# Attention with projections: the transposing transfers of the softmax sums move to ScalarE's queue

## The chip, the cores and the metric

The kernel runs on one core of a Trainium2 chip. Its five engines (TensorE for matmuls, VectorE, ScalarE, GpSimd, and SyncE, which here only issues transfers) each work through their own list of instructions in order and wait for one another through semaphores. The metric is the device time of one execution in microseconds (us). A profiled execution is a little longer than an unprofiled one, so profiles are compared with profiles and times with times. In the profile's rows PE is TensorE, PEld its weight loads, DVE VectorE, ACT ScalarE, POOL GpSimd, SPq the transfers that SyncE issues and ACTq those that ScalarE issues. L939 is line 939 of the kernel.

## What is computed

One attention block on a picture of 48 x 48 = 2304 positions with 512 channels and a batch of 4, in 8 heads of 64 channels. Cut to what matters:

```python
hn  = group_norm(x, gn_scale, gn_bias)                 # 32 groups
qkv = einsum('oc,bchw->bohw', qkv_w, hn) + qkv_b       # fp32, then rounded to fp16
q, k, v = (qkv[:, i] for i in range(3))                # each (b, 8, 64, 2304)
w   = einsum('bhct,bhcs->bhts', q * scale, k * scale)  # scale = 64 ** -0.25
w   = softmax(w, axis=-1)
a   = einsum('bhts,bhcs->bhct', w, v)
out = x + einsum('oc,bchw->bohw', proj_w, a) + proj_b
```

## The kernel before

The kernel takes two heads at a time: 16 pairs of heads, each with five blocks of columns (positions t), four of 512 columns and a last one of 256. The exponentials of a block are made in *bursts* of three tiles of 128 x 1024. A block of 512 columns has six bursts, the one of 256 has three, and a pair has 27. Projections for later pairs and for the output ("pieces") are put between the bursts, so that TensorE is always busy.

The softmax's sums don't come from TensorE. VectorE adds up the exponentials (`add`), which leaves for each column 128 partial sums, one in each partition. A transposing transfer (`turn`) moves them so that VectorE can reduce them along a row (`sum_up`); then come the reciprocal and a detour through DRAM that spreads it over the partitions (`invert`, `spread`), and GpSimd's multiplication (`divide`).

```python
ppool = tile_pool(name="ppool", bufs=3)               # exponentials, one buffer a burst
ps_s  = tile_pool(name="ps_s", bufs=3, space=PSUM)    # scores, one buffer a tile
ps_w  = tile_pool(name="ps_w", bufs=1, space=PSUM)    # projections: one bank
...
def scores(u):
    ...
    for r in range(BURST):                            # BURST = 3
        ps = ps_s.tile([P, 2, QB], F32, tag="ps")
        ...                                           # 2 (or 4) matmuls into ps
        nc.scalar.activation(pt[:, r], ps, AF.Exp)
...
def add(u):                                           # "acc", and at the block's end "j"
    ...
    nc.vector.tensor_tensor(t, before, pt, ALU.add)
    if last:
        whole = work.tile([P, 1, 2, QB], F16, tag="joined", bufs=1)
        ...                                           # two additions of 128 x 1024
...
def turn(g, j):
    t = work.tile([P, 2 * QB // P, P], F16, tag="turned", bufs=1)
    (whole,) = acc.pop((g, j))
    nc.sync.dma_start(t, whole.rearrange("p a h q -> p (a h q)"), transpose=True)
    turned[g, j] = t

def sum_up(g, j):                                     # L1038 (512 columns), L1041 (256)
    sm = small.tile([P, 2, QB // P], F32, tag="sums")
    ...
    nc.vector.tensor_reduce(sm, t[:, :, :, 0], AX.X, ALU.add)
...
def invert(g, j):
    nc.vector.reciprocal(inv[:, :, :per], sums[g, j][:, :, :per])
    row = dram.tile([2, QB], F32, tag="row")
    for h in range(2):                                # writes of 4 bytes each
        nc.sync.dma_start(row[h, :n].rearrange("(i p) -> p i", p=P), inv[:, h, :per])

def spread(g, j):                                     # one row over 64 partitions
    ib = work.tile([P, QB], F32, tag="ib", bufs=1)
    for h in range(2):
        nc.sync.dma_start(ib[h * D : (h + 1) * D, :n], row[h : h + 1, :n].to_broadcast((D, n)))

def divide(g, j):
    nc.gpsimd.tensor_tensor(atts[g][:, o : o + n], avx[g, j], ibs[g, j], ALU.mult)
```

The order in which each engine gets its work, burst by burst (`n` counts the bursts of all pairs; `block_at(m)` is the block that ended with burst `m`, if one did):

```python
for n in range(end):
    ...                               # loads and stores that are due
    if block_at(n - 3):
        turn(*block_at(n - 3))
    ...
    scores(stream[n])                 # TensorE and ScalarE, burst n
    add(stream[n - 1])                # VectorE
    values(stream[n - 2])             # TensorE; copies av out at a block's end
    fill(n)                           # small VectorE tasks, then projection pieces
    if block_at(n - 4):
        sum_up(*block_at(n - 4)); check_sums(...); invert(...)
    if block_at(n - 6):
        spread(*block_at(n - 6))
    if block_at(n - 7):
        divide(*block_at(n - 7))
```

A piece of the projections is a chain of matmuls into the one bank of `ps_w`, which VectorE empties (k and q at L719, v at L768, the output's residual sum `r` at L864).

Of the kernel before, what the change touches and what calls it, by code (L numbers as in the profile page):

```python
# [33 lines left out]
BEHIND = 2  # L34
# [10 lines left out]
NQ = len(QBLOCKS)  # L45
# [422 lines left out]
def fast_path(  # L468
# [12 lines left out]
    nc = tc.nc  # L481
# [438 lines left out]
    def scores(u):  # L920
        g, j, k, _ = u
        o, n = QBLOCKS[j]
        per = QB // n
        qt, kt = qk[g]
        pt = ppool.tile([P, BURST, 2, QB], F16, tag="p", name=f"p_{g}_{j}_{k}")
        for r in range(BURST):
            ps = ps_s.tile([P, 2, QB], F32, tag="ps", name=f"ps_{g}_{j}_{k}_{r}")
            for a in range(per):
                i = (k * BURST + r) * per + a
                for h in range(2):  # L930
                    rows = slice(h * D, (h + 1) * D)
                    nc.tensor.matmul(  # L932
                        ps[:, h, a * n : (a + 1) * n],
                        kt[rows, bass.ts(i, P)],
                        qt[rows, o : o + n],
                        start=True,
                        stop=True,
                    )
            nc.scalar.activation(pt[:, r], ps, AF.Exp)  # L939
        pts[u] = pt  # L940
# [27 lines left out]
    def add(u):  # L968

        g, j, k, last = u  # L970
        pt = pts[u]
        if k == 0:
            acc[g, j] = [pt]
            return
        if j >= NQ - 2 and g == NG - 1 and (last or j == NQ - 1):
            acc[g, j].append(pt)
            return
        before = acc[g, j][0]
        if k == 1:
            acc[g, j] = [  # L980
                work.tile(
                    [P, BURST, 2, QB], F16, tag="acc", bufs=1, name=f"acc_{g}_{j}"
                )
            ]
        t = acc[g, j][0]
        nc.vector.tensor_tensor(t, before, pt, ALU.add)  # L986
        if last:
            whole = work.tile([P, 1, 2, QB], F16, tag="joined", bufs=1, name=f"j_{g}_{j}")
            so_far = t[:, 0]
            for r in range(1, BURST):  # L990
                nc.vector.tensor_tensor(whole[:, 0], so_far, t[:, r], ALU.add)
                so_far = whole[:, 0]
            acc[g, j] = [whole]
# [30 lines left out]
    def turn(g, j):  # L1024


        t = work.tile([P, 2 * QB // P, P], F16, tag="turned", bufs=1, name=f"t_{g}_{j}")
        (whole,) = acc.pop((g, j))
        nc.sync.dma_start(t, whole.rearrange("p a h q -> p (a h q)"), transpose=True)
        turned[g, j] = t  # L1030

    def sum_up(g, j):

        o, n = QBLOCKS[j]
        sm = small.tile([P, 2, QB // P], F32, tag="sums", name=f"sums_{g}_{j}")
        t = turned[g, j].rearrange("p (h a i) k -> p h i a k", h=2, i=n // P)
        if n == QB:
            nc.vector.tensor_reduce(sm, t[:, :, :, 0], AX.X, ALU.add)  # L1038
        else:
            for h in range(2):  # L1040
                nc.vector.tensor_reduce(sm[:, h, : n // P], t[:, h], AX.XY, ALU.add)  # L1041
        sums[g, j] = sm
# [21 lines left out]
    def check_sums(g, j):  # L1064
        n = QBLOCKS[j][1]
        sm = sums[g, j][:, :, : n // P]
        ok = fine.rearrange("p (h i) -> p h i", h=2)[:, :, : n // P]
        for op, limit in ((ALU.is_ge, SUM_MIN), (ALU.is_le, SUM_MAX)):
            t = small.tile([P, 2, QB // P], F32, tag="in", name=f"in_{g}_{j}")
            t = t[:, :, : n // P]  # L1070
            nc.gpsimd.tensor_scalar(t, sm, limit, None, op)  # L1071
            nc.gpsimd.tensor_tensor(ok, ok, t, ALU.mult)  # L1072

    def invert(g, j):
        n = QBLOCKS[j][1]
        per = n // P
        inv = small.tile([P, 2, QB // P], F32, tag="inv", name=f"inv_{g}_{j}")
        nc.vector.reciprocal(inv[:, :, :per], sums[g, j][:, :, :per])
        row = dram.tile([2, QB], F32, tag="row", name=f"row_{g}_{j}")
        if (g, j) in turned:  # L1080
            for h in range(2):
                nc.sync.dma_start(  # L1082
                    row[h, :n].rearrange("(i p) -> p i", p=P), inv[:, h, :per]
                )
        else:
            nc.sync.dma_start(
                row[:, :n].rearrange("h (p i) -> p h i", i=per), inv[:, :, :per]
            )
        rowd[g, j] = row

    def spread(g, j):
        n = QBLOCKS[j][1]
        row = rowd.pop((g, j))
        ib = work.tile([P, QB], F32, tag="ib", bufs=1, name=f"ib_{g}_{j}")
        for h in range(2):
            nc.sync.dma_start(
                ib[h * D : (h + 1) * D, :n], row[h : h + 1, :n].to_broadcast((D, n))
            )
        ibs[g, j] = ib

    def divide(g, j):
        o, n = QBLOCKS[j]
        nc.gpsimd.tensor_tensor(  # L1103
            atts[g][:, o : o + n],
            avx.pop((g, j))[:, :n],
            ibs.pop((g, j))[:, :n],
            ALU.mult,
        )
# [37 lines left out]
    def do_tasks(room):  # L1146
        while tasks and tasks[0][0] <= now[0] and room > 0:
            _, us, run = tasks.popleft()
            run()
            room -= us  # L1150
# [18 lines left out]
    def ready(b, j):  # L1169

        if b < B - 1:
            return BEHIND + 7
        return BEHIND + (4 if j == NQ - 3 else 6)

    def put_convert(b, j):
        end = ends[((b + 1) * NPAIR - 1) * NQ + j]
        put(projs[b, j][0], end + ready(b, j))
# [130 lines left out]
    def issue():  # L1308
        us, run = beside.pop(0)[:2]
        run()  # L1310
        credit[0] -= us

    def fill(n):

        idle = beside and beside[0][4] and not beside[0][4]()
        if ended(n - 1):
            room = 1.1 if idle else 0.0  # L1320
        elif ended(n - 4):
            room = 1.1 if idle else 0.3
        else:
            room = 2.4 if idle else 1.1
        do_tasks(room)
        rate, work = 0.0, 0.0
        for us, _, _, _, _, _, need in beside:
            work += us
            left = min(need * per_pair, len(stream) - 4) - n
            rate = max(rate, work / max(left, 1))  # L1330
        credit[0] = min(credit[0] + rate, 4.0)
        closed = False
        while beside:
            us, _, first, last, when, after, _ = beside[0]
            if after > n or (first and closed) or (when and not when()):
                break
            if us > 0.1 and credit[0] < us / 2:
                break
            issue()
            closed = closed or last  # L1340

    def wanted(g):

        while any(p[6] <= g for p in beside):
            while loads:
                loads.popleft()[1]()
            while tasks:
                tasks.popleft()[2]()
            issue()
            credit[0] = max(credit[0], 0.0)  # L1350

    ended = lambda n: 0 <= n < len(stream) and stream[n][3]
# [5 lines left out]
    def block_at(n):  # L1358

        return stream[n][:2] if ended(n) and n not in soon else None  # L1360

    for n in range(end):
        now[0] = n
        while loads and loads[0][0] <= n:
            loads.popleft()[1]()
        if block_at(n - 3):
            turn(*block_at(n - 3))
        wanted(stream[n][0])
        scores(stream[n])
        if n > 0:  # L1370
            add(stream[n - 1])
        if n >= BEHIND:
            values(stream[n - BEHIND])
        fill(n)

        if block_at(n - 4):
            sum_up(*block_at(n - 4))
            check_sums(*block_at(n - 4))
            invert(*block_at(n - 4))
        if block_at(n - 6):  # L1380
            spread(*block_at(n - 6))
        if block_at(n - 7):

            divide(*block_at(n - 7))
        if n - BEHIND in soon:
            g, j = stream[n - BEHIND][:2]
            sx = rows(g, j, add_up(g, j))
            if n - BEHIND == soon[1]:
                divide_here(g, j, sx, avx[g, j], nc.gpsimd)
        if n - BEHIND - 1 == soon[0]:  # L1390
            check_sums(g, j)
            invert(g, j)
        if n - BEHIND - 2 == soon[0]:
            spread(g, j)
            divide(g, j)
    g, b, j = NG - 1, B - 1, NQ - 1
    n = QBLOCKS[j][1]
# [99 lines left out]
```

## Time and profile before

| | |
|---|---|
| time, median of 3 runs | 1739.31 us (1738.06 to 1740.24) |
| span of the profiled execution | 1777.9 us |
| mean clock granted to TensorE in it | 0.959 of full speed |
| bursts | 432 |
| transposing transfers | 77, all issued by SyncE |
| exponentials, 128 x 1024 | 1296, mean 1026 ns |
| transfers of reciprocals into DRAM rows | 155 |

A row of the profile's list of groups gives line, engine, operation, what is written from what, the shape and the count; then the busy time, the mean duration of one in ns, and the idle time just before with what ended most of it. The list of waits names the waiting engine and line, then what it waited for, the total in us, the number of times and the longest. A row of the timeline has the start, the duration, the engine, the line and the operation; in brackets stand the idle time before it and what ended it. The duration of a transfer's command is the time in which it was issued, not the time until its data had landed; the latter can be read in the chain of waits, where a DMA row lasts until its data let the next instruction start.

### The profile page before, as it was taken

What the parts mean: (1) busy time and instruction counts of PE and PEld (TensorE: products, weight loads), DVE (VectorE), ACT (ScalarE), POOL (GpSimd) and SP (SyncE); (2) the same over time, 40 slices, a digit from 0 to 9 for tenths busy, and PEclk for the clock granted to TensorE, in tenths of its full rate; (3) what the DMA queues carried; (4) which work ended last, traced back from release to release, by engine and by line L of the source; (5) the groups of instructions that cost most, each with busy time, mean ns of one, the idle gap of its engine ahead of it and who ended that gap; (6) DMA issues with size and microseconds to landing.
All of it is one profiled execution on the core that took longest, in us unless ns stands there. A gap on an engine that the chain in (4) does not pass through costs nothing.

```text
span 1777.9 us, 27819 instructions
## 1 busy us (share of the span) xinstructions
PE 1609.6 (91%) x11316; PEld 700.4 (39%) x11316; DVE 1193.8 (67%) x1317; ACT 1285.4 (72%) x1398; POOL 340.2 (19%) x419
## 2 busy tenths in 40 slices
PE   7999999999999977899999999669999989987677
PEld 2533434433335334453333443335333335334344
DVE  5277677777676766766767667667676767655565
ACT  3287777888878865676878788548787878876575
POOL 1011212221121211112223121111222231210111
PEclk9999999999999997999999999879999999999789
DMA  6012151211111367613111115562312212168534
GB/s 201 1 43 53 22 84 27 32 25 22 37 22 31 72 107 108 108 25 34 25 34 25 31 31 107 109 120 45 40 25 30 29 22 25 34 115 130 85 54 127
DMA packets 206718, 101.97 MB, mean 57 GB/s; under 512 B 162676, under 2 KB 172788, under 8 KB 206580
## 3 DMA queue, kind: packets, MB, share of 16 engines
q1 hardware_dynamic: 204548, 98.25, 31.5%
q8 instruction: 90, 1.47, 0.5%
q10 hardware_dynamic: 1904, 1.84, 0.3%
q14 instruction: 48, 0.39, 0.1%
q0 software_dynamic: 128, 0.01, 0.0%
HBM read 60.70 MB, written 19.17 MB: 45 GB/s over the span
## 4 chain that ended last, share of the span: by engine, by line
PE 62%; DMA 21%; DVE 10%; issue 3%; ACT 2%; SPq 2%; POOL 0%; DVEq 0%; ACTq 0%; POOLq 0%
PE pqk L709 20%; PE ps L932 12%; PE av L957 12%; PE pv L760 11%; DMA t<-j 10%; DMA r<-x_dram 7%; PE pr L837 6%; DVE acc L986 3%; DMA row<-inv 2%; DMA x<-x_dram 2%; DVE sums L1038 2%; ACT p L939 1%; PE ps L709 1%; DVE r L864 1%; SPq L1082 1%
## 5 line engine op out<-in xcount | busy, mean ns | idle before, releaser
L939 ACT ACTIVATE p<-ps 128x1024 f16<-128x1024 f32 x1296 | 1232.3, 1026 | 432.1 <-PE ps L932 419.5
L709 PE MATMUL pqk<-x,wqkv 128*64 128x512 f32 (+1 forms) x2464 | 526.8, 558 | 29.3 <-DVE k L719 14.8
L986 DVE TENSOR_TENSOR acc<-acc,p 128x3072 f16<-128x3072 f16 x270 | 488.2, 1808 | 34.1 <-ACT p L939 31.1
L932 PE MATMUL ps<-q,k 64*128 64x512 f16 (+1 forms) x2880 | 366.0, 364 | 6.6 <-ACT p L939 5.9
L957 PE MATMUL av<-p,v 128*64 128x512 f16 (+1 forms) x2880 | 364.5, 367 | 1.9 <-DVE avx L966 1.5
L760 PE MATMUL pv<-wqkv,x 128*64 128x256 f32 x2304 | 271.3, 383 | 12.4 <-DVE v L768 11.9
L709 PEld LDWEIGHTS pqk<-x,wqkv 128*64 128x64 f32 x2464 | 172.8, 139 | 253.3 <-issue 166.4
L1103 POOL TENSOR_TENSOR att<-avx,ib 128x512 f16<-128x512 f32 (+1 forms) x78 | 122.4, 1570 | 714.6 <-DMA ib<-row 669.2
L932 PEld LDWEIGHTS <-k 64*128 64x128 f16 x2880 | 108.2, 95 | 321.7 <-issue 274.9
L837 PE MATMUL pr<-a,whi 128*128 128x512 f32 (+1 forms) x312 | 134.5, 437 | 96.1 <-DVE r L864 93.1
L1071 POOL TENSOR_SCALAR in<-sums 128x8 f32<-128x8 f32 (+1 forms) x158 | 92.2, 584 | 655.3 <-DVE sums L1038 437.5
L957 PEld LDWEIGHTS <-v 128*64 128x64 f16 x2880 | 126.6, 109 | 215.3 <-issue 176.3
L760 PEld LDWEIGHTS pv<-wqkv,x 128*64 128x64 f32 x2304 | 161.9, 138 | 103.9 <-DVE v L768 14.8
L986 DVE TENSOR_TENSOR acc<-p,p 128x3072 f16<-128x3072 f16 x79 | 140.3, 1776 | 17.5 <-ACT p L939 16.4
L864 DVE SCALAR_TENSOR_TENSOR r<-pr,bproj,r 128x512 f32<-128x512 f32 (+1 forms) x80 | 54.8, 693 | 131.8 <-DMA r<-x_dram 84.9
L837 PE MATMUL pr<-a,wlo 128*128 128x512 f32 (+1 forms) x312 | 125.6, 408 | 0.0
L837 PEld LDWEIGHTS pr<-a,whi 128*128 128x128 f32 x312 | 65.6, 210 | 136.5 <-DVE r L864 74.2
L1072 POOL TENSOR_TENSOR fine<-fine,in 128x8 f32<-128x8 f32 (+1 forms) x158 | 114.5, 725 | 13.2
L719 DVE TENSOR_SCALAR q<-pqk,bqkv 128x512 f16<-128x512 f32 (+1 forms) x79 | 54.8, 694 | 82.4 <-PE pqk L709 81.9
L768 DVE TENSOR_TENSOR v<-pv,bv 128x512 f16<-128x512 f32 x72 | 49.6, 689 | 88.3 <-PE pv L760 82.6
L719 DVE TENSOR_SCALAR k<-pqk,bqkv 128x512 f16<-128x512 f32 (+1 forms) x75 | 52.2, 696 | 70.7 <-PE pqk L709 69.5
L966 DVE COPY avx<-av 128x512 f32<-128x512 f32 (+1 forms) x79 | 49.9, 631 | 53.8 <-PE av L957 48.7
(66 smaller groups left out, 526.9 us busy)
## 6 DMA issues: line engine op xcount, KB each, us to landing
r<-x_dram SPq DMA_DIRECT2D x72, 256.0 KB
out_dram<-r SPq DMA_DIRECT2D x69, 256.0 KB
ib<-row SPq DMA_DIRECT2D x126, 128.0 KB
x<-x_dram SPq DMA_DIRECT2D x62, 256.0 KB
x<-x_dram SPq DMA_DIRECT2D x16, 128.0 KB
row<-inv SPq DMA_DIRECT2D x124, 2.0 KB
ib<-row SPq DMA_DIRECT2D x30, 64.0 KB
wqkv<-qkv_wT_dram SPq DMA_DIRECT2D x2, 768.0 KB
```

The costliest lines, as they stand in the source:

```text
L709: nc.tensor.matmul(pw[0][lo : lo + D, :n], wqkv[:, c, w0 + lo : w0 + lo + D], hn[b, c, j], start=(c == 0), stop=(c == NC - 1),)
L719: nc.vector.tensor_scalar(qk[g][part][:, o : o + n], pw[0][:, :n], bqkv[:, col : col + 1], SCALE, ALU.add, ALU.mult,)
L760: nc.tensor.matmul(pw[0][lo : lo + D, a, :], hn[b, c, i * P // QB][:, at + lo : at + lo + D], wqkv[:, c, 2 * C + half * C // 2 :][:, : C / ...
L837: nc.tensor.matmul(ps[:, :n], w[:, c, bass.ts(m, P)], at32[b, j, c], start=(i == 0), stop=(i == len(steps) - 1),)
L864: nc.vector.scalar_tensor_tensor(xt[:, i], places[i], bias, xt[:, i], ALU.add, ALU.add)
L932: nc.tensor.matmul(ps[:, h, a * n : (a + 1) * n], kt[rows, bass.ts(i, P)], qt[rows, o : o + n], start=True, stop=True,)
L939: nc.scalar.activation(pt[:, r], ps, AF.Exp)
L957: nc.tensor.matmul(av[0][lo : lo + D, :n], vv[b, pr // 2][:, i, pr % 2 * P + lo : pr % 2 * P + lo + D], pt[:, r, h, a * n : (a + 1) * n], ...
L986: nc.vector.tensor_tensor(t, before, pt, ALU.add)
L1071: nc.gpsimd.tensor_scalar(t, sm, limit, None, op)
L1072: nc.gpsimd.tensor_tensor(ok, ok, t, ALU.mult)
L1103: nc.gpsimd.tensor_tensor(atts[g][:, o : o + n], avx.pop((g, j))[:, :n], ibs.pop((g, j))[:, :n], ALU.mult,)
```

## The change

The transposing transfers go into ScalarE's list instead of SyncE's. There they stand ahead of the exponentials of the burst that is three after their block's last one. Everything that hangs on them follows one burst later: VectorE's sums with GpSimd's check and the reciprocal, the spreading, the division, and the moment at which the output's projection may take the block. The amount of small tasks that VectorE gets in the burst of the sums is moved along. The purpose is to take the transposing transfer out of the queue in which it stands behind scattered writes and waiting transfers, and to give it time to land before VectorE reaches the sum.

```diff
@@ def turn(g, j)
-        nc.sync.dma_start(t, whole.rearrange("p a h q -> p (a h q)"), transpose=True)
+        nc.scalar.dma_start(t, whole.rearrange("p a h q -> p (a h q)"), transpose=True)
@@ def ready(b, j)
         if b < B - 1:
-            return BEHIND + 7
-        return BEHIND + (4 if j == NQ - 3 else 6)
+            return BEHIND + 8
+        return BEHIND + (4 if j == NQ - 3 else 7)
@@ def fill(n)
         if ended(n - 1):
             room = 1.1 if idle else 0.0
-        elif ended(n - 4):
+        elif ended(n - 5):
             room = 1.1 if idle else 0.3
@@ for n in range(end)
-        if block_at(n - 4):
-            sum_up(*block_at(n - 4))
-            check_sums(*block_at(n - 4))
-            invert(*block_at(n - 4))
-        if block_at(n - 6):
-            spread(*block_at(n - 6))
-        if block_at(n - 7):
-            divide(*block_at(n - 7))
+        if block_at(n - 5):
+            sum_up(*block_at(n - 5))
+            check_sums(*block_at(n - 5))
+            invert(*block_at(n - 5))
+        if block_at(n - 7):
+            spread(*block_at(n - 7))
+        if block_at(n - 8):
+            divide(*block_at(n - 8))
```

## The prediction

> **What bounds the kernel now.** I read the page first, then the waits, then the stretch around one short block in the order of time. The page's engine shares and the chain:
>
> ```profile
> PE 1609.6 (91%) x11316; PEld 700.4 (39%) x11316; DVE 1193.8 (67%) x1317; ACT 1285.4 (72%) x1398; POOL 340.2 (19%) x419
> ...
> PE 62%; DMA 21%; DVE 10%; issue 3%; ACT 2%; SPq 2%; POOL 0%; DVEq 0%; ACTq 0%; POOLq 0%
> ```
>
> TensorE works 91% of 1777.9 us, so everything that a change can win lies in its 168 us of idle time (26 of them in the first 100 us and after 1740). The list of waits says who ends that idle time:
>
> ```profile
> PE pr L837 <- DVE r L864: 93.1, 15, 9.1
> ...
> DVE sums L1041 <- DMA t<-j: 61.6, 13, 9.3
> ...
> PE pqk L709 <- DVE k L719: 14.8, 7, 4.0
> ...
> PE pv L760 <- DVE v L768: 11.9, 5, 3.8
> ...
> PE pqk L709 <- DVE q L719: 11.0, 5, 4.6
> ...
> DVE sums L1038 <- DMA t<-j: 4.2, 3, 1.9
> ```
>
> The 93.1 us are projections waiting for VectorE to add a residual that is still loading; the change doesn't aim there. The next three TensorE rows are waits for VectorE to empty a PSUM bank. Their origin is the DVE row of 61.6 us: VectorE stands still for the turned sums of the pair's last block (L1041 is the form for 256 columns), 13 times, up to 9.3 us. One of them in the order of time (start, duration, engine, line):
>
> ```profile
> 379.29 1.21 DVE L1038 TENSOR_REDUCE sums<-t 128x8 f32<-128x1024 f16 x1
> ...
> 380.76 0.93 SPq L1082 DMA_DIRECT2D row<-inv  x2
> ...
> 381.42 0.48 DVE L719 TENSOR_SCALAR k<-pqk,bqkv 128x256 f16<-128x256 f32 x1 [0.39 <-PE pqk L709]
> ...
> 381.73 1.23 SPq L1029 DMA_TRANSPOSE t<-j  x1
> ...
> 392.08 1.28 DVE L1041 TENSOR_REDUCE sums<-t 128x2 f32<-128x512 f16 x2 [3.29 <-DMA t<-j]
> ...
> 395.14 0.74 DVE L719 TENSOR_SCALAR q<-pqk,bqkv 128x512 f16<-128x512 f32 x1
> ...
> 395.94 1.94 PE L709 MATMUL pqk<-x,wqkv 128*64 128x512 f32 x8 [1.61 <-DVE q L719]
> ...
> 398.24 2.85 ACT L939 ACTIVATE p<-ps 128x1024 f16<-128x1024 f32 x3 [2.22 <-PE ps L932]
> ```
>
> The last block has three bursts instead of six, so its transposing transfer (381.73) comes on SyncE right behind the previous block's two scattered writes (380.76). It lands some 10.3 us after its issue, VectorE has waited 3.29 us for it, then empties the bank late, and TensorE loses 1.61 us, ScalarE with it.
>
> How late depends on what stands ahead in the queue. In the chain of waits a transfer behind such writes takes 9.35 to 11.5 us, one without them 4.5 to 6:
>
> ```profile
> 263.14 10.00 DMA row<-inv
> ...
> 381.73 10.33 DMA t<-j
> ...
> 619.65 4.46 DMA t<-j
> ...
> 892.54 6.06 DMA t<-j
> ```
>
> **What the Trainium skill says.** "DMA: Bandwidth & Descriptors", section "Queues, rings and completion order": SyncE and ScalarE each own one row of rings on the same 16 DMA engines, and each engine goes round-robin between rows. So in ScalarE's row the transpose needn't wait behind SyncE's 4-byte writes. The two groups of landing times above fit a queue that holds it up. The same page, "Issuing engines are not separate DMA queues", says that a second issuer saves only the issuing time; taken strictly that speaks against a faster landing (a rival below). "Perfetto Trace Analysis", section on the DVE and Act engine instruction: an activation is pushed into a wait queue and the sequencer goes on to the next instruction, so a command may be handled while earlier activations run. Its section on the HWDGE DMA instruction: the sequencer itself waits for a transfer's semaphores and is taken until the descriptors are made. The trace has 1.25 us (median of 77) for that on SyncE; ScalarE issues nothing in its steady state here, so its share isn't shown.
>
> **The change part by part.** The number and form of all compute instructions stay, and so does TensorE's order; 77 transposes move from SyncE's list into ScalarE's, three bursts after their block ended, ahead of that burst's exponentials; the sums move one burst down VectorE's list, behind one more addition and often one more bank.
>
> *Taken away.* I went through the DVE waits for t and added the TensorE gaps that follow within 14 us, nearly all with VectorE emptying a bank as releaser: 1.4, 2.9, 1.6, 3.7, 1.7, 4.0, 2.4, 2.4, 3.8, 3.2, 4.6 and 3.1, together 34.8 us for twelve short blocks. The thirteenth (9.35 us wait, 8.6 us gap) is among the projections; 93.1 / 15 = 6.2 us is usual there, so I count 2.5. Two of the L1038 waits have gaps of 1.4 and 1.3: count 2. Together 39 us. A burst is 3.25 us where projections run beside it, which with the lost queue (10.3 down to about 5 or 6) covers waits of 3.2 to 6.2 us. I take all of it off.
>
> *Added, one: a wait of ScalarE.* The tile t has one buffer. The short block's transpose must follow the sum over the block before. That sum used to stand a burst earlier; now it stands at the end of the burst right ahead of this transpose, in 11 of 15 pairs directly after the emptying of a bank. From the end of TensorE's chain: 0.1 + 0.75 (k, 694 to 750 ns) + 1.21 (the sum) = 2.1 us, then 1.25 us of issuing: the next exponential starts 3.35 us after the chain's end. Now it starts 0.45 after (0.38 to 0.45 in the timeline). There are three score tiles, so TensorE needs the third of the burst free 3.25 + 0.55 us after the chain's end, and three exponentials take 2.86: a start up to 0.9 costs nothing, one at 3.35 costs 2.4. Where two pieces of projection stand in that burst (as at 382.73, 3.60 us), or a projection's wait, most of it is swallowed. I count 8 pairs at 1.7, 3 at 0.5 and 4, with no bank in between, at 0.4: 17 us.
>
> *Added, two: the issuing itself.* 77 x 1.25 = 96 us of ScalarE's sequencer, against 28% of idle ScalarE. For the 62 transposes of long blocks the sums joined are 3 to 6 us old and t is free. If the sequencer runs ahead, one exponential or two (0.95 us each) hide the issue. If not, the start moves from 0.45 to 1.4 and costs 0.5: 31 us at most. I weigh full exposure with a quarter: 8 us.
>
> *Moved.* Row writes, broadcast and division come a burst later. In the projection stages a residual behind row writes takes 11 to 13 us; as many row writes stand among as many residual loads as before, only one place later. I count 0, plus or minus 10. The tail isn't touched: the last block that is turned has its division at 1724.2 and its conversion at 1735.0.
>
> Sum: -39 + 17 + 8 + 0 = -14 us, so about 1725 us.
>
> **The rivals.** (1) *The full gain.* The wait on t's buffer is mostly swallowed and the issue hidden: -39 to -45, 1697 us. For it: ScalarE is only 72% busy. Against it: in the very bursts concerned it has 0.4 us of slack in 3.25. (2) *ScalarE as the new wait.* It isn't able to run ahead, every transpose blocks 1.25 us and the short ones over 3: -39 + 31 + 26 = +18, 1757 us; with slower issuing than on SyncE still more. For it: the queue is in order and TensorE has only three score tiles. Against it: TensorE's mean burst is about 3.8 us (1640 us by 432 bursts) while the exponentials need 2.86. (3) *The landing stays slow* at 10 us, because the same 16 engines are busy with the small writes. Then the added burst of 3.25 us still takes away most of the waits of 3.2 to 4.2, but not those over 5: some 12 us of gain are missing, 1737 us. (4) *The gain is given back to the residuals.* SyncE reaches its loads at the same time, TensorE reaches its projections earlier and waits longer for them: the 93 us become 105. It is inside my plus or minus 10.
>
> **Range and chances.** 1725 us, with 1702 to 1752 for 8 in 10: its lower end is the full gain with little given back, its upper end nearly rival (2). 2% are 34.8 us: under 1704.5 needs nearly all of the gain and none of the two additions, 0.12; over 1774 needs exposed issuing much above 1.25 us or ScalarE waiting for other transfers, 0.06; within 2%, 0.82.
>
> **What would show it.** *Right:* the row of DVE waiting for t, 61.6 us, falls below 10; transposes of short blocks are issued 2 us after the chain's end and have landed within 6 or 7; TensorE's 38 us of waits for k, q and v shrink; a new row appears, ScalarE's exponential or its transposing command waiting for DVE sums, some 1 to 2 us in each of 10 or more pairs, with TensorE's scores waiting for ScalarE (5.9 us now) at 15 to 30. *The issuing:* the gap between exponentials before and after a transpose of a long block, 0.4 us if hidden, 1.4 or more if not. *Wrong:* if that gap is far above 1.4, or DVE's wait for t stays above 30, or the projections' 93.1 us move by more than 15.

## The result: slower by 1.5%

| kernel | time, median | ratio to the kernel before, 95% interval |
|---|---|---|
| before | 1738.68 us (1735.41 to 1740.24, 4 runs) | |
| changed | 1764.36 us (1762.93 to 1765.55, 4 runs) | 1.015 [1.0132, 1.0167] |

About 26 us are lost where 14 were to be won. The change did what it was made for, and something else took more than that back.

One caution on levels. The kernel before takes 1738.7 us on the chip of this table and 1764.4 us on the chip of most experiments below, 1.5% apart for the same program. The profile of before that was shown above has a span of 1777.9 us and belongs to neither level. Profiling as such is not the reason: the changed kernel's profiled execution took 1765.15 us, within its range in the table. So ratios are formed on one chip only, and the trace of the change is compared with a repeat of the kernel before (`e0_before_again`) from the same chip as the repeat of the change (`e4_after_again`).

### The profile page after: what moved, and what is told of

Its sections match the earlier page's. It is cut to its first block, busy times and chain, and to the rows that moved or that the text cites. A ratio compares the mean times of both kernels' runs of the same rounds, so it can differ in the third digit from the quotient of the medians.

```text
span 1763.4 us, 27868 instructions
## 1 busy us (share of the span) xinstructions
PE 1613.5 (91%) x11316; PEld 703.9 (40%) x11316; DVE 1185.7 (67%) x1317; ACT 1284.1 (73%) x1398; POOL 359.0 (20%) x419
## 4 chain that ended last, share of the span: by engine, by line
PE 69%; DMA 13%; DVE 8%; ACT 4%; issue 4%; ACTq 1%; SPq 1%; POOL 0%; DVEq 0%; POOLq 0%
PE pqk L709 22%; PE av L957 14%; PE ps L932 13%; PE pv L760 12%; PE pr L837 6%; DMA r<-x_dram 5%; ACT p L939 4%; DMA row<-inv 3%; DMA t<-j 3%; DVE sums L1038 2%; DVE acc L986 2%; PE ps L709 1%; DMA out_dram<-r 1%; DVE r L864 1%; ACTq L1029 1%
## 5 line engine op out<-in xcount | busy, mean ns | idle before, releaser
L986 DVE TENSOR_TENSOR acc<-acc,p 128x3072 f16<-128x3072 f16 x270 | 478.9, 1774 | 74.5 <-ACT p L939 72.3
L932 PE MATMUL ps<-q,k 64*128 64x512 f16 (+1 forms) x2880 | 369.8, 362 | 48.0 <-ACT p L939 47.3
L957 PE MATMUL av<-p,v 128*64 128x512 f16 (+1 forms) x2880 | 369.6, 371 | 5.6 <-DVE slx L1048 4.2
L1071 POOL TENSOR_SCALAR in<-sums 128x8 f32<-128x8 f32 (+1 forms) x158 | 87.4, 553 | 653.4 <-DVE sums L1038 482.3
L864 DVE SCALAR_TENSOR_TENSOR r<-pr,bproj,r 128x512 f32<-128x512 f32 (+1 forms) x80 | 54.8, 694 | 132.0 <-PE pr L837 59.0
L1072 POOL TENSOR_TENSOR fine<-fine,in 128x8 f32<-128x8 f32 (+1 forms) x158 | 137.1, 867 | 13.2
```

Source lines behind the costliest of these rows:

```text
L864: nc.vector.scalar_tensor_tensor(xt[:, i], places[i], bias, xt[:, i], ALU.add, ALU.add)
L932: nc.tensor.matmul(ps[:, h, a * n : (a + 1) * n], kt[rows, bass.ts(i, P)], qt[rows, o : o + n], start=True, stop=True,)
L957: nc.tensor.matmul(av[0][lo : lo + D, :n], vv[b, pr // 2][:, i, pr % 2 * P + lo : pr % 2 * P + lo + D], pt[:, r, h, a * n : (a + 1) * n], ...
```

## The profile after

The page of the changed kernel, its engine shares and its chain of waits:

```profile
PE 1613.5 (91%) x11316; PEld 703.9 (40%) x11316; DVE 1185.7 (67%) x1317; ACT 1284.1 (73%) x1398; POOL 359.0 (20%) x419
...
PE 69%; DMA 13%; DVE 8%; ACT 4%; issue 4%; ACTq 1%; SPq 1%; POOL 0%; DVEq 0%; POOLq 0%
```

The chain has moved: DMA down from 21% to 13%, ScalarE up from 2% to 4% (on one chip, `e0_before_again` and `e4_after_again`, from 20% to 16% and from 1% to 4%), and ScalarE's sequencer (ACTq) is in it with 1%. Which waits stand behind that is read from the lists of waits of the two kernels on one chip. First the kernel before:

```profile
PE pr L837 <- DVE r L864: 87.0, 15, 8.4
...
DVE sums L1041 <- DMA t<-j: 57.1, 13, 8.7
...
PE pqk L709 <- DVE k L719: 13.4, 6, 3.6
...
PE pv L760 <- DVE v L768: 10.8, 5, 3.5
...
PE pqk L709 <- DVE q L719: 9.4, 5, 3.7
...
PE ps L932 <- ACT p L939: 4.5, 10, 0.5
```

and then the changed kernel:

```profile
PE pr L837 <- DVE r L864: 71.1, 14, 7.9
...
ACT p L939 <- issue: 57.7, 15, 7.5
...
PE ps L932 <- ACT p L939: 50.2, 65, 7.4
...
DVE avx L966 <- POOL att L1103: 20.9, 12, 5.3
...
PE av L957 <- DVE avx L966: 7.4, 4, 2.8
...
DVE sums L1041 <- DMA t<-j: 6.7, 6, 2.5
...
PE av L957 <- DVE slx L1048: 5.0, 1, 5.0
...
PE pv L760 <- DVE v L768: 2.4, 5, 0.8
...
PE pqk L709 <- DVE k L719: 1.8, 4, 1.0
...
PE pqk L709 <- DVE q L719: 0.6, 3, 0.2
```

VectorE's wait for t is gone (57.1 to 6.7 us), and with it TensorE's waits for k, q and v. In their place ScalarE's exponentials wait 57.7 us for nothing that the profile names ("issue": here its own sequencer, held at a transfer's command), and TensorE's scores wait 50.2 us for ScalarE. Two smaller rows are new as well: VectorE copies av out late because GpSimd's division, a burst later, still reads the tile (20.9 us), and TensorE waits for that.

The balance of this pair, TensorE's gaps between 100 and 1740 us summed from the rows of the timeline by what ended them (0.1 us beside the lists here and there):

| TensorE waits for | before | changed | difference |
|---|---|---|---|
| k, q, v out of the bank | 36.9 | 6.4 | -30.5 |
| the residual sums r | 87.3 | 71.0 | -16.3 |
| the exponentials | 4.6 | 50.2 | +45.6 |
| avx, slx (copies of av and of its sums) | 1.7 | 12.4 | +10.7 |
| all gaps | 130.5 | 140.1 | +9.6 |
| TensorE's busy time | 1608.5 | 1616.7 | +8.2 |

The spans are 1763.9 and 1782.7 us, 18.8 apart; the table holds 17.8 of it.

Two stretches of the changed kernel's timeline, from the profile with the page above, show how a transposing transfer stands among the exponentials, first a long block's, then a short block's:

```profile
374.33 1.02 ACT L939 ACTIVATE p<-ps 128x1024 f16<-128x1024 f32 x1 [0.39 <-PE ps L932]
...
374.85 1.25 ACTq L1029 DMA_TRANSPOSE t<-j  x1
...
375.25 1.94 ACT L939 ACTIVATE p<-ps 128x1024 f16<-128x1024 f32 x2
...
387.81 1.21 DVE L1038 TENSOR_REDUCE sums<-t 128x8 f32<-128x1024 f16 x1
...
389.05 1.31 ACTq L1029 DMA_TRANSPOSE t<-j  x1
...
390.46 5.61 ACT L939 ACTIVATE p<-ps 128x1024 f16<-128x1024 f32 x6 [3.46 <-issue]
...
393.36 0.39 PE L932 MATMUL ps<-q,k 64*128 64x512 f16 x2 [0.51 <-ACT p L939]
...
400.20 1.27 DVE L1041 TENSOR_REDUCE sums<-t 128x2 f32<-128x512 f16 x2
```

For the long block the command (374.85) starts while the first of three exponentials runs, and the next two follow without a gap: issuing is hidden. For the short block the command (389.05) comes 0.03 us after the sum over the block before has ended (387.81 + 1.21), and so it is at all fifteen short blocks of `e4_after_again`: it has waited for the one buffer of t, and ScalarE's next exponential stands still for 3.46 us. The sum over the short block at 400.20 then waits for nothing, 11.15 us after the command.

## The experiments

They ran on three chips: the runs from e0 to e7 on one on which the kernel before took 1764 us, e8 to e10 on another of the same level (1763.9 us), the last on a third. "TensorE waits for exponentials" and the like are sums as in the table above, on each run's own trace.

**The kernel before, again.** No edit; it gives the trace to compare with.

> The kernel before, unchanged, profiled once more. The first profile of it had a span of 1777.9 us beside times of 1739 us; that of the changed kernel had 1763.4 us beside 1764. Theory A (the profiled execution of before was later than its timed ones because transfers landed later in it, so that its 61.6 us of VectorE waiting for the turned sums are not what a timed execution has): another profile has a span near 1739, VectorE's wait for t under 25 us, and TensorE's waits for k, q and v together under 20 instead of 38. Theory B (the profile was typical and the change itself costs 25 us somewhere else): the span is again about 1778 and the waits are the same.

Measured 1764.35 us, ratio 1.0002 [0.9985, 1.0019]; span 1763.9, granted clock 0.961. Theory A falls: VectorE's wait for t is 57.1 us, TensorE's for k, q and v 37.0. The waits that the prediction built on are typical. The span of 1763.9 us fits neither theory.

**The changed kernel, again.** No edit; is the loss the same on the other chip?

> The changed kernel, unchanged, beside many runs of the kernel before on one and the same chip. In the first three experiments' call the kernel before itself took 1764.5 us where it had taken 1738.7 for the result. Theory A2 (the chip or its state makes 1.5% of the kernel's time, and the change itself is nearly neutral, its gain of about 54 us in TensorE's waits for VectorE given back in about 43 us of waits for ScalarE): 0.995 to 1.003 of the kernel before in this call. Theory A1 (the change costs 1.5% on any chip): 1.012 to 1.018.

Measured 1784.8 us, 1.0122 [1.0098, 1.0145]. The loss belongs to the change and not to a chip.

**The later burst alone.** The changed kernel, transposing transfers back on SyncE:

```diff
-        nc.scalar.dma_start(t, whole..., transpose=True)
+        nc.sync.dma_start(t, whole..., transpose=True)
```

> The changed kernel with the transposes back in SyncE's queue, so only the burst of delay is left. Theory A (what costs is ScalarE, which stands in its own queue until the sum over the long block before is made, 3.3 us in each pair, while the waits for t were small in timed executions): 1725 to 1742 us, at or below the kernel before, and no gaps of 3.3 us between exponentials. Rival C (the later sums, divisions and conversions cost the 25 us, whatever queue issues): 1755 to 1770 us. Rival D (residual loads fall into a worse place behind the row writes): TensorE's waits for VectorE at L864 above 80 us.

Measured 1769.25 us, 1.003 [1.0018, 1.0043]. Theory A, with the kernel before or below, is out, and so is rival C, since the later burst alone costs 5 us and not 25; rival D's sign (80.0 us at L864) says nothing, with 87.0 in the kernel before. A burst more does not cure the wait here, since SyncE too must wait for t's buffer; it issues later, and VectorE then waits a second time, for the joined tile that the transfer reads:

```profile
DVE sums L1041 <- DMA t<-j: 36.3, 12, 7.1
...
DVE j L991 <- DMA t<-j: 26.6, 10, 7.8
```

TensorE's waits for k, q and v are 37.0 us, as before the change; those for avx and slx 9.7 us instead of 1.7. That is what the later burst brings by itself.

**ScalarE's queue alone.** The kernel before with only the other line of the change:

```diff
-        nc.sync.dma_start(t, whole..., transpose=True)
+        nc.scalar.dma_start(t, whole..., transpose=True)
```

> The kernel before with only the queue changed; sums stay four bursts after their block. ScalarE then finds t free earlier in the short blocks, but the sum over the short block itself comes a burst earlier. Theory A: ScalarE's stalls at the short blocks shrink from 3.3 to about 1 us, VectorE waits for t a little (10 to 30 us in all), time 1740 to 1755. Rival E (issuing from ScalarE costs as such): 1760 or more, with gaps of 1.3 us or more at the long blocks too.

Measured 1752.28 us, 0.9929 [0.9905, 0.9952]. VectorE's wait for t falls to 39.0 us (10 to 30 were expected), TensorE waits 11.1 us for exponentials. So 0.7% is won by one half of the change, 0.3% lost by the other, and 1.2% lost by the two together: the loss lies in how they act on each other.

The trace of this run takes a belief of the prediction away. In the twelve cases in which VectorE waits for a short block's transfer, the time from the command to the sum's start is the landing time. It is 9.4 to 11.2 us on SyncE's queue (`e0_before_again`, without the one at 1105 us, among the loads) and 9.9 to 12.8 us on ScalarE's. The other queue does not make it land sooner; VectorE only waits less because the command goes out earlier.

**The fourth block's sum back in its old burst.** The changed kernel; only the long block just ahead of the short one gets its sum, check and reciprocal a burst earlier, so that t is free when ScalarE comes to the short block's transfer:

```diff
-        if block_at(n - 5):
-            sum_up(...); check_sums(...); invert(...)
+        for due in (4, 5):
+            found = block_at(n - due)
+            if found and (due == 4) == (found[1] == NQ - 2):
+                sum_up(*found); check_sums(*found); invert(*found)
```

> The changed kernel with one thing put back: the sum over the fourth block, which has to free t for the short block's transpose, is again four bursts after its block. Theory A: the 3.3 us stalls of ScalarE at the short blocks fall to under 1, TensorE's waits for exponentials fall from 47 to about 15 us, and the time falls by 20 to 35 us to 1730 to 1745. Rivals C and E: it stays within 8 us of 1764.

Measured 1757.26 us, 0.996 [0.9948, 0.9972], against 1.0122 with the sum late: 1.6% by this one edit. The 3.3 us stalls at short blocks are gone from the trace, VectorE's wait for t stays small (7.3 us), and TensorE's wait for exponentials falls from 50.2 to 28.4 us, not to 15. Of what is left most stands in the stages in which the next picture is loaded, and looks the same as in the changed kernel: exponentials that wait 6.0 and 7.8 us at 618 and 650 us.

**The picture's loads off SyncE.** Those remaining stalls needed a cause. One of them in the timeline of the changed kernel (`e4_after_again`):

```profile
652.55 2.50 SPq L1096 DMA_DIRECT2D ib<-row  x2
...
656.20 2.55 SPq L512 DMA_DIRECT2D x<-x_dram  x4
...
658.67 1.25 ACTq L1029 DMA_TRANSPOSE t<-j  x1
659.20 1.26 POOL L1103 TENSOR_TENSOR att<-avx,ib 128x512 f16<-128x512 f32 x1 [15.72 <-DMA ib<-row]
660.02 2.85 ACT L939 ACTIVATE p<-ps 128x1024 f16<-128x1024 f32 x3 [7.54 <-issue]
661.10 0.61 PE L932 MATMUL ps<-q,k 64*128 64x512 f16 x2 [7.41 <-ACT p L939]
```

The transposing command starts 0.53 us before GpSimd begins to use `ib`, the broadcast that SyncE issued at 652.55 and that has nothing to do with t. The compiled program's own list of waits says why (cut to the transfers between the two). DMAHW0 to DMAHW7 are the eight completion semaphores, counters that a transfer raises when its data has landed; the transfers of SyncE and ScalarE take them in turn:

```
SyncE    ib_1   <- row_1    [waits DMAHW6, DMAHW4, Pool]
SyncE    ib_1   <- row_1    [waits DMAHW7, DMAHW5]
SyncE    r_0_0  <- x_dram   [waits PE]
SyncE    r_0_1  <- x_dram   [waits PE]
SyncE    x_0_3  <- x_dram   [waits DMAHW0]
SyncE    x_1_3  <- x_dram   [waits DMAHW1]
SyncE    x_2_3  <- x_dram   [waits DMAHW2]
SyncE    x_3_3  <- x_dram   [waits DMAHW3]
ScalarE  t_2    <- j_2      [waits DMAHW5, DMAHW4, DVE]
```

A transfer waits until the last user of its semaphore has landed. The transposing transfer is the eighth after the first half of the broadcast and takes the same one, DMAHW4.

The trace holds this wait too, as an instruction of ScalarE's sequencer ahead of each of the 77 commands (the durations are the shortest, the median and the longest in ns):

```profile
L1029 ACTq EVENT_SEMAPHORE  x77: 17/38/8079, 103.4 to 1706.0; - x77
```

The one of this place waits from 650.57 to 658.63, and the last update of DMAHW4, the landing of the broadcast's first half, stands at 658.61. The longest (1091.68 to 1099.76) ends in the same way with a broadcast that landed at 1099.74. At the third long stall, which ends at 628.19, the eighth transfer before is the write of the previous block's reciprocals: it landed at 625.82, and the command started at 625.91. Four smaller stalls at long blocks (131, 237, 260 and 1075 us, with 6.4 us of TensorE after them) also end with the landing of such a write.

If the shared semaphore costs the time, taking the loads out of the count must help the changed kernel, and must do next to nothing for the kernel before:

```diff
 def load_block(b, j):
     for c in range(NC):
-        load_x(b, j, c, nc.sync)
+        load_x(b, j, c, nc.gpsimd)
```

> The changed kernel with the later batches' input loads issued by GpSimd instead of SyncE. Each SyncE or ScalarE transfer reuses the completion semaphore of the one eight transfers earlier, and in the stages with input loads that is the previous block's spreading transfer, still in flight: ScalarE stood 8.3, 6.5 and 5.4 us there. With the loads off these semaphores the eighth transfer back is an old one. Theory F (that is what ScalarE waits for): the three stalls fall below 2 us, TensorE's waits for exponentials fall from 47 to about 30 us, time 8 to 17 us less than the changed kernel in the same call. Rival G (ScalarE waits there for the joined sums or for t): the stalls stay.

> The same for the kernel before, to tell what the input loads' queue does without ScalarE's transposes. Theory F: within 6 us of the kernel before (its transposes are in SyncE's list, where nobody computes). If it gains 10 us or more, then the shorter SyncE queue is what helps the run before this one too.

> The input loads issued by GpSimd and the fourth block's sum four bursts after its block, both on the changed kernel: no ScalarE stall over 2 us should be left at the short blocks or in the loading stages. Theories A and F together: TensorE's waits for exponentials under 15 us, 0.98 to 0.99 of the kernel before. If it isn't below the run with the early sum alone (0.996), F falls.

Measured: 1.0038 [1.0017, 1.0059] for the changed kernel with it (1.0122 without), 0.9987 [0.9975, 0.9999] for the kernel before with it, 0.9939 [0.9921, 0.9956] together with the fourth block's early sum (0.996 without). In the changed kernel with this edit the transposing transfer of this place waits for two other semaphores, and its command goes out together with the broadcast's, not after its landing:

```profile
650.49 2.05 SPq L1096 DMA_DIRECT2D ib<-row  x2
650.57 2.26 ACTq L1029 DMA_TRANSPOSE t<-j  x1
...
652.92 5.61 ACT L939 ACTIVATE p<-ps 128x1024 f16<-128x1024 f32 x6 [0.52 <-ACT a L831]
```

The three long stalls of the loading stages (6.0, 7.5 and 7.1 us, 17.6 us of TensorE) are gone, and the four smaller ones too; TensorE's wait for exponentials is 28.7 us, and 12.8 us with both edits. With both, 0.98 to 0.99 had been expected; 0.9939 misses that, but lies below 0.996 as theory F needed.

**The same for the best half of the change.** ScalarE's queue alone, with the picture's loads on GpSimd:

> The kernel before with two edits only: the transposing transfers issued by ScalarE, the picture's loads issued by GpSimd; nothing a burst later. If ScalarE's stalls in the loading stages come from a transposing transfer waiting for the transfer eight places ahead on SyncE and ScalarE together, taking the loads out of that count helps here too: 0.986 to 0.991 of the kernel before, and TensorE's wait for the exponentials falls from 11.1 us to 4 to 6. If they are nothing but the short blocks' hold of t, this kernel stays at the 0.993 of the one with ScalarE's queue alone.

A miss: 1761.14 us, 0.9985 [0.9967, 1.0002], worse than without (0.9929, on the other chip of this level). TensorE's wait for exponentials did fall, from 11.1 to 6.4 us, but its waits for k, q and v rose from 22.8 to 35.4. Loads on GpSimd are a way to take the stalls away, and they have a price of their own; why those waits rise is open.

**Only the short block later.** What the runs so far ask for: ScalarE issues the transposing transfers, only the pair's last block has its sum, broadcast and division a burst later, with the moment at which the output's projection may take it, and nothing else is moved. (The transfer also stands ahead of the burst's loads in the program.)

```diff
+        for late in (0, 1):
+            def found(m, late=late):
+                at = block_at(m - late)
+                return at if at and late == (at[1] == NQ - 1) else None
-        if block_at(n - 4):
-            sum_up(...); check_sums(...); invert(...)
-        if block_at(n - 6):
-            spread(...)
-        if block_at(n - 7):
-            divide(...)
+            if found(n - 4):
+                sum_up(...); check_sums(...); invert(...)
+            if found(n - 6):
+                spread(...)
+            if found(n - 7):
+                divide(...)
```

> ScalarE issues the transposing transfers, and only the pair's last, short block has its sum, broadcast and division a burst later; the four long blocks keep the place of before, and the transfer stands ahead of a burst's loads. Theory: only the short block's sum came too early, and only the fourth block's late sum held t. Then VectorE's 57 us of waits for t fall below 12 as with the change, no exponential waits 3.3 us at short blocks, VectorE's and TensorE's waits for the GpSimd multiplications and the shifts (11 us more with the change) are mostly gone: 0.984 to 0.990. The rival, that the loading stages cost what they cost with the change: about 0.996, as with the early sum of the fourth block.

> The same with the picture's loads issued by GpSimd. Theory of the count of eight: 2 to 6 us faster than without, 0.982 to 0.988, TensorE's wait for the exponentials below 8 us. Rival, that the order of transfer and loads in the list has already removed the stalls: the same time as without, within 0.2%.

Measured 1731.22 us, 0.9808 [0.9784, 0.9832], the best of all and better than expected; with the loads on GpSimd 1738.8 us, 0.9853 [0.9826, 0.988], slower than without and so a miss in the same direction as above, though inside the ratio that was expected. The list of waits of the run without them on GpSimd:

```profile
PE pr L837 <- DVE r L864: 85.3, 15, 9.1
...
PE ps L932 <- ACT p L939: 11.4, 21, 2.8
...
DVE avx L966 <- POOL att L1103: 7.4, 3, 4.1
...
DVE sums L1041 <- DMA t<-j: 4.5, 4, 2.9
...
PE pqk L709 <- DVE k L719: 3.5, 3, 1.6
```

The change's gain is there (VectorE's wait for t 4.5 us, TensorE's for k, q and v 10.4 in all), and its price is not. The shared semaphore is still there, but the broadcast stands a burst further ahead of the transfer and comes nearly in time:

```profile
626.74 1.35 SPq L1096 DMA_DIRECT2D ib<-row  x2
...
632.42 1.56 ACTq L1029 DMA_TRANSPOSE t<-j  x1
...
632.96 1.26 POOL L1103 TENSOR_TENSOR att<-avx,ib 128x512 f16<-128x512 f32 x1 [15.63 <-DMA ib<-row]
634.08 5.61 ACT L939 ACTIVATE p<-ps 128x1024 f16<-128x1024 f32 x6 [2.94 <-DVE k L719]
```

Again the command starts 0.54 us before GpSimd takes `ib`, but the exponential stalls 2.94 us instead of 7.54. (The profile puts this down to k; ScalarE's sequencer waited for the semaphores from 629.23 to 632.38.) So the change's later spreading also took part in the loss: it brought the broadcast up to the transfer with which it shares a semaphore.

Not all of the 1.9% lies in waits. The spans of this trace and of `e0_before_again` are 32.0 us apart, TensorE's gaps (as in the table) 16.8 and its busy time 12.5. The record of the granted clock has stretches at half speed: 22 of them with 87.6 us of TensorE's work in the kernel before, 14 with 63.8 us here. By estimate half of this difference, 12 us, is time lost to half speed. Six of the stretches that are gone (at 305, 492, 817, 1240, 1339 and 1431 us) begin within 1.3 us of the end of a gap of 2.9 to 3.7 us that TensorE has just after VectorE's wait at a short block. So a removed gap may save more than its own length; that the gaps bring the stretches about was not tested.

**The transfer ahead of the loads.** The changed kernel with two statements exchanged, to move the transfer in the count of eight; it ran on a chip on which the kernel before took 1737.26 us:

```diff
+        if block_at(n - 3):
+            turn(*block_at(n - 3))
         while loads and loads[0][0] <= n:
             loads.popleft()[1]()
-        if block_at(n - 3):
-            turn(*block_at(n - 3))
```

> The changed kernel with one edit: in each burst the transposing transfer stands ahead of the loads in the program's order, not behind them. Its sums stay a burst later, so the short blocks' hold of t stays (about 16 us of TensorE in ten pairs). Theory of the count of eight: the three stalls of ScalarE in the loading stages (6.0, 7.5 and 7.1 us, 17.6 us of TensorE together) go, because the transfer eight places ahead is then an old one: 1.000 to 1.006 of the kernel before, and TensorE's wait for the exponentials falls from 50 to about 30 us. Rival, that these stalls come from the traffic of the loads, whatever the order: 1.010 to 1.014 and the wait stays at 45 to 50.

Measured 1763.6 us, 1.0154 [1.0129, 1.018], with the stalls in place (5.5, 6.9 and 6.4 us). This settles nothing between the two theories, because the edit did not do what was meant: in the compiled program the transposing transfer of the place shown above still waits for DMAHW5 and DMAHW4, like the unedited one. It shows that the order of these two statements changes nothing, so that it has no part in the 0.9808 either, and repeats the loss of the change on this chip.

## Why the prediction was wrong

*Taken away, 39 us.* Right in the main, and for a partly wrong reason. The waits for k, q and v lost 30.5 us where 34.8 and 2 were counted. The row of VectorE waiting for t fell below 10 as said. But "landed within 6 or 7" is wrong: the six waits that are left show landings of 10.4 to 12.3 us. The lost queue made no transfer land sooner; rival (3) had that right, but not its consequence: with the command early enough, a burst more covers even 12 us. The Trainium skill had said so where the prediction made it a mere rival: "DMA: Bandwidth & Descriptors", section "Issuing engines are not separate DMA queues", lets a second issuer save only the time of issuing. The landings of 9.4 to 11.2 us on one queue and 9.9 to 12.8 on the other agree with it. What makes a short block's transfer slow was not measured.

*Added, one, 17 us.* Right in mechanism and size. Of the changed kernel's 15 stalls in the row of "issue", ten stand at short blocks, mostly 3.3 to 3.9 us long, with 15.1 us of TensorE after them.

*Added, two, 8 us.* This is the step that failed. Its first question, whether 1.25 us of issuing are exposed, has the answer 0 where its semaphores are free: the sequencer runs ahead. But the step, and the sentence that for long blocks "t is free", took t and the issuing for all that a command can wait for. It also waits for the earlier transfer that has the same completion semaphore, and on ScalarE this holds the exponentials as well. Three such stalls took 17.6 us of TensorE, the four smaller ones 6.4 more: 24.0 us, where 8 were counted for issuing. On SyncE only other transfers stand behind such a wait. The prediction named ScalarE "waiting for other transfers" only as a tail of 0.06. The skill's page on DMA, section "Anatomy of one DMA — SWDGE (gpsimd) path", has the piece that mattered: a transfer's semaphore waits are made by the issuing sequencer, not by the DMA engines. The prediction had this piece as well; it did not ask which semaphores they are. "Perfetto Trace Analysis", section "DMA Instruction — HWDGE (DVE, Sync)", says that the reported window begins only when they are satisfied. So it looks in this trace: the command's row in the timeline has 1.25 us, and the wait ahead of it appears there only as part of ScalarE's 7.54 us of idle time, "issue".

*Moved, 0 plus or minus 10.* This step failed with the one above: it asked only what the later writes and broadcasts do to the residual loads. These writes and broadcasts are the transfers that the transposing ones then had to wait for. The residuals gave 16.3 us back (87.3 to 71.0), more than the margin and by the prediction's own words a sign of error; why was not tested. Against it stand 10.7 us of waits for avx and slx that no step had. The run with the later burst alone has 9.7 us of them and the kernel with only the short block later 3.0: with the long blocks' division late but the fourth sum early it is 9.1. So they come from dividing the long blocks later.

*The sum.* By the terms as measured: -30.5 - 16.3 + 45.6 + 10.7 = +9.5 us of gaps. The changed kernel's 50.2 us of waits for exponentials hold 15.1 of the kind that had been predicted and 24.0 of the shared semaphore; the rest are smaller waits that were not taken apart, with 4.6 in the kernel before. Another 8.2 us are TensorE's busy time, for the same matmuls at the same granted clock (0.961 and 0.960). By the estimate used above, the stretches at half speed (90.0 us of work in them against 87.6) explain 1.2 of it. The cause of the rest stays open. Over all the runs busy time went from 1596.0 us (the best kernel, clock 0.967) to 1616.7 (the changed one, 0.960); by the same estimate half speed has 13 of those 21 us.

*Rivals.* (2) gave the nearest time, by luck: ScalarE did become the new wait, but not by issuing.

## What to carry to other kernels

Before a transfer's command goes to a computing engine, list everything that the command itself waits for: its buffer's last reader, and the transfer whose completion semaphore it takes over. All of it will hold the instructions behind it. Delay only the consumer that comes too early: here a burst for one block in five wins 1.9%, and the same burst for all five, with the same queue, loses 1.2%.

## What the hardware and the program showed that was not expected

- Transfers of SyncE and ScalarE share eight completion semaphores in this compiled program, so a transfer can wait for one of the other engine, of other data, eight places before: 7.54 us of ScalarE at 660 us, in which its sequencer waited for that landing and then issued.
- ScalarE's transposing commands for long blocks cost nothing where their semaphores are free: they start some 0.5 us into the first exponential of the burst before.
- The same program is 1.5% apart on two chips (1738.7 and 1764.4 us), as much as the whole effect; only ratios on one chip tell anything. The mean granted clock differs too, 0.963 on the chip of 1764 us and 0.971 on that of 1737.26 us. If all of TensorE's busy time followed that clock, which was not shown, it would make 13 of the 27 us, by estimate from 1608.5 us of busy time.
